# Selective scan on one core: one 1024-column scan over two channel quarters, with a zero decay standing at their border

## The chip, the cores and the metric

The kernel runs on one NeuronCore of one Trainium2 chip. The time is the device time of one execution in microseconds (us). Six instruction streams matter: PE (TensorE, matmuls), DVE (VectorE), ACT (ScalarE), POOL (GpSimd), SP (which issues most transfers), and the transfers themselves. Each engine works through its own queue in the order in which the program lists the instructions, and waits at the head of its queue until what the instruction needs is there.

## The reference, cut to what matters

Four layers run one after another: attention with group norm, a deformable convolution block, three residual convolution steps, and a four-direction state-space layer (Mamba). The change touches the last one only. For a token sequence of L = 4096 positions, 256 inner channels and 16 states per channel it computes

```python
dA  = jnp.exp(dt[..., None] * A)                         # decay, between 0 and 1
dBu = dt[..., None] * Bm[:, :, None, :] * xh[..., None]
def step(h, inp):
    dA_t, dBu_t = inp
    h = dA_t * h + dBu_t
    return (h, h)
_, hs = lax.scan(step, h0, (dA..., dBu...))              # h0 = 0
y = jnp.einsum('lbdn,bln->bld', hs, Cm)
```

for 2 images and 4 directions (rows and columns, each forward and flipped). The sequence starts at zero in each direction.

## The kernel before

**Tiling.** In `layer3` a block is 512 positions (`BLK`) of one direction of one image: 64 blocks, 8 per direction. The state goes from one block to the next of the same direction. Within a block the 256 channels fall into two halves (`hf`) of 128, and the 16 states into four sets (`ng`) of 4. A *group* is (block, half, set), so there are 8 groups in a block, and `slot` is the number of the group in its block. The 128 partitions of a group's tile hold 4 states x 32 channels; the four quarters `q` of a half's 128 channels lie side by side along the free dimension. The tile `db` (128 x 4 x 512) holds all of a group.

**What happens to a group.**
- `spread_store` and `spread_load` bring dt (and dt times u) by way of DRAM (`dx`) into the tile `dd4`, in which each channel's row stands four times.
- `db_dve` (L1518, the product at L1522) and `db_pool` (L1527, L1531) write the products dBu into `db`. The table `ND` (L1239) says how many of the 512 columns are DVE's; the rest are POOL's. Three groups have a POOL share: slot 1 and slot 6 entirely, slot 2 from column 176. DVE's share reads B from a PSUM tile `pbc`, which a matmul in `weights` (L1494, L1501) writes; POOL's reads a copy `b` fetched by SP.
- `expo` (L1541) lets ACT write the decays of one quarter into a PSUM tile `da` (L1544). There are three `da` buffers, and ACT runs two quarters ahead of DVE (`AHEAD`, L1695).
- `scan` (L1552, L1558) is one DVE instruction for 512 columns of one quarter. It reads `da` and `db` and writes the states into `db`. The state at the end of the block before enters in one of two ways: as the scan's starting value, read from `hl`, or, where `carried` (L1536) says so, by a small ACT instruction in `expo` (L1550) that adds decay times `hl` to the first column of `db`; the scan then starts from zero.
- `keep` (L1560, L1563) copies the last column to `hl` on ACT.
- `cmul` (L1565, L1568) multiplies the states by C on POOL, and `sums` (L1570, L1576) adds the states of a channel by small matmuls into `py`; `gate` (L1582, L1585) multiplies the result by the silu of z on DVE.

**What sets the order.** The layer is written under a manual schedule: each engine's queue has the order of the Python calls. The main loop (L1749) takes one group `k` per round. A round issues transfers for the next block, `weights(k + 2)`, then for each quarter an exponential (two quarters ahead) and a scan; then `db_dve(k + 1)`, `cmul(k - 1)`, `db_pool(k + 2)`; then one portion of the front of the next block by `slot` (`front_pe`, `front_act`, `front_pool`: projections, softplus, silu); and last `sums(k - 2)`. Among ACT's portions are `conv_silu` in slot 7 (L1409) and `zproj_silu` in slot 4 (L1422), each with two loads of the activation table, and `softplus` in slots 1 and 2. In some blocks one more tile of layer norm for a later block is worked in (13 in the main loop); its mean and variance take `da` buffers (`ln_tile`, L1320).

**PSUM** has 8 banks of 512 columns: `da` 3, `pbc` 2, `py` 1, and `pm3` 2 for all else in the layer.

Of the kernel before, what the change touches and what calls it, by code (L numbers as in the profile page):

```python
# [1229 lines left out]
def layer3(g, I, out):  # L1230
# [5 lines left out]
    nc, tc = g.nc, g.tc  # L1236
    NJ = 4

    ND = ((BLK, 0, 176, BLK), (BLK, BLK, 0, BLK))  # L1239
    NNG = N_STATE // NJ  # L1240
    HB = 1
    HC = 3
    with ExitStack() as ctx:
        a = ctx.enter_context(tc.tile_pool(name="l3a", bufs=1))
        dr = ctx.enter_context(tc.tile_pool(name="l3dr", bufs=2, space=bass.MemoryType.DRAM))
        psd = ctx.enter_context(tc.tile_pool(name="l3psd", bufs=3, space=PSUM))
        psb = ctx.enter_context(tc.tile_pool(name="l3psb", bufs=2, space=PSUM))
# [67 lines left out]
        xt = a.tile([P, L + 2 * HC], F32, name="xt")  # L1315
        N = {}
        NFIRST = 3


        def ln_tile():  # L1320

            return psd.tile([P, BLK], F32, name="da")

        def ln_mean(b, k):
            N[k, "mean"] = ln_tile()
            nc.tensor.matmul(N[k, "mean"], onesm, interior(g, b, k * RB, RB), start=True, stop=True)

        def ln_less(b, k):
# [10 lines left out]
            nc.scalar.activation(N[k, "sq"], N[k, "xc"], AF.Square)  # L1339

        def ln_var(b, k):
            N[k, "var"] = ln_tile()
# [42 lines left out]
        def reverse(i):  # L1385
            b, nd, _ = blocks[i]
            return dirs[b][nd][2]
# [91 lines left out]
        def spread_store(i, hf):  # L1479

            S[i]["dx", hf] = dr.tile([P, 2, BLK], F32, name="dx")
            nc.sync.dma_start(S[i]["dx", hf], S[i].pop(("dd", hf)))

        def spread_load(i, hf):
            s_ = S[i]
            dx = s_.pop(("dx", hf))
            dd4 = d4.tile([P, 2, 4, BLK], F32, name="dd4")
            for x in range(2):
                src = dx[:, x, :].rearrange("(q c) t -> c q t", c=32)
                for j in range(NJ):  # L1490
                    nc.sync.dma_start(dd4[32 * j : 32 * j + 32, x], src)
            s_["d4", hf] = dd4

        def weights(k):  # L1494

            i, hf, ng = groups[k]
            G[k] = {}
            if ND[hf][ng] == 0:
                return
            pb = psb.tile([P, BLK], F32, name="pbc")  # L1500
            nc.tensor.matmul(pb, sel[:, ng].rearrange("p j c -> p (j c)"), S[i]["bc"], start=True, stop=True)  # L1501
            G[k]["pb"] = pb
# [8 lines left out]
                nc.sync.dma_start(t[32 * j : 32 * j + 32], S[i]["bx"][r0 + j].partition_broadcast(32))  # L1511

        def db_tile(k):
            if "db" not in G[k]:
                G[k]["db"] = wk.tile([P, 4, BLK], F32, name="db")
            return G[k]["db"]

        def db_dve(k):  # L1518
            i, hf, ng = groups[k]
            n = ND[hf][ng]  # L1520
            if n:
                nc.vector.tensor_tensor(  # L1522
                    db_tile(k)[:, :, :n], G[k].pop("pb")[:, :n].unsqueeze(1).to_broadcast([P, 4, n]),
                    S[i]["d4", hf][:, 1, :, :n], ALU.mult,
                )
# [7 lines left out]
                    S[i]["d4", hf][:, 1, :, n:], ALU.mult,  # L1533
                )

        def carried(k, q):  # L1536

            i, hf, ng = groups[k]
            return i % NBLK > 0 and (q >= 2 or ND[hf][ng] == 0)

        def expo(k, q):  # L1541
            i, hf, ng = groups[k]
            da = psd.tile([P, BLK], F32, name="da")
            nc.scalar.activation(da, S[i]["d4", hf][:, 0, q, :], AF.Exp, scale=am[:, hf, q, ng : ng + 1])  # L1544
            G[k]["da", q] = da
            if carried(k, q):

                first = BLK - 1 if reverse(i) else 0
                b0 = G[k]["db"][:, q, first : first + 1]
                nc.scalar.activation(b0, da[:, first : first + 1], AF.Identity, bias=b0, scale=hl[:, hf, ng, q, :])  # L1550

        def scan(k, q):  # L1552
            i, hf, ng = groups[k]
            d0, d1 = G[k].pop(("da", q)), G[k]["db"][:, q, :]
            if reverse(i):
                d0, d1 = d0[:, ::-1], d1[:, ::-1]
            zero = i % NBLK == 0 or carried(k, q)
            nc.vector.tensor_tensor_scan(d1, d0, d1, 0.0 if zero else hl[:, hf, ng, q, :], ALU.mult, ALU.add)  # L1558

        def keep(k):  # L1560
            i, hf, ng = groups[k]
# [75 lines left out]
        def transfers(i, slot):  # L1637
            if i < NBK:
                if slot == 1:
                    bc_store(i)  # L1640
                elif slot == 4:
                    spread_store(i, 0)
                elif slot == 5:
                    spread_load(i, 0)
                    spread_store(i, 1)
            if slot == 0 and i - 1 < NBK:
                spread_load(i - 1, 1)
            for x, ahead in (("b", 4), ("c", 1)):
# [37 lines left out]
        with tc.manual_schedule():  # L1686
# [7 lines left out]
            units = [(k, q) for k in range(len(groups)) for q in range(4)]  # L1694
            AHEAD = 2  # L1695

            for k in range(NFIRST):
                ln_mean(0, k)
            for k in range(NFIRST):
# [34 lines left out]
            for ng in range(NNG):  # L1734
                copies(0, "b", ng)
                copies(0, "c", ng)
            for k in range(2):
                weights(k)
            db_dve(0)
            db_pool(0)  # L1740
            front_pe(0, 4)
            front_act(0, 4)
            front_pe(0, 5)
            front_pe(0, 6)
            for u in range(AHEAD):
                expo(*units[u])
            front_act(0, 7)
            db_pool(1)
            for k in range(len(groups) + 7):  # L1749
                i, slot = divmod(k, 8)  # L1750
                live = k < len(groups)
                more = k + 1 < len(groups)
                ended = 1 <= k <= len(groups)
                transfers(i + 1, slot)
                if k + 2 < len(groups):
                    weights(k + 2)
                norm = next_norm(i)
                for q in range(4):
                    if slot == 6 and q == 3 and 1 <= i <= NBK:
                        finish(i - 1)  # L1760
                    if norm and slot == 2 and q == 3:
                        ln_log(*norm)
                    if q == 0 and ended:
                        keep(k - 1)
                    if 4 * k + q + AHEAD < len(units):
                        expo(*units[4 * k + q + AHEAD])
                    if norm and q == 0:
                        if slot == 0:
                            ln_mean(*norm)
                        elif slot == 2:  # L1770
                            ln_var(*norm)
                    if live:
                        scan(k, q)

                    for j, hf in (((k - 6) // 8, 0), ((k - 10) // 8, 1)):
                        if q == 1 and 8 * j + 6 + 4 * hf == k and 0 <= j < NBK:
                            gate(j, hf)
                if norm and slot == 0:
                    ln_less(*norm)
                if more:  # L1780
                    db_dve(k + 1)
                if ended:
                    cmul(k - 1)
                if k + 2 < len(groups):
                    db_pool(k + 2)

                if slot == 5 and 0 <= k - 2 < len(groups):
                    sums(k - 2)
                if slot == 5 and 1 <= i <= NBK:
                    project(i - 1)  # L1790
                front_pe(i + 1, slot)
                front_act(i + 1, slot)
                front_pool(i + 1, slot)
                if norm:
                    if slot == 1:
                        ln_square(*norm)
                    elif slot == 3:
                        ln_root(*norm)
                    elif slot == 5:
                        ln_scale(*norm)  # L1800
                    elif slot == 6:
                        ln_store(*norm)
                if live:

                    if slot == 6 and 0 < i % (4 * NBLK) <= NBLK // 2:
                        for n in range(2):
                            turn(blocks[i][0], 2 * (i % (4 * NBLK) - 1) + n)

                if slot != 5 and 0 <= k - 2 < len(groups):
                    sums(k - 2)  # L1810


@with_exitstack
# [157 lines left out]
```

## Time and profile before

| | us |
|---|---|
| median of 3 runs | 5605.49 (5605.03 to 5607.73) |
| the profiled execution | 5610.11 |
| its span in the trace | 5608.3 |
| scan stage in the trace, first to last scan | 2309.25 to 5593.16 |
| DVE busy from 2309 to 5594 | 3207.1 |
| POOL busy there | 3236.5 |
| ACT busy there | 2777.5 |
| PE busy there | 2627.1 |

The profile is one execution. Its page gives the busy time of each engine, then the span in 40 slices with a digit for the busy tenths, then the chain of work that ended last, then groups of instructions: line, engine, operation, tiles (out<-in), shapes, count, then busy us in total and mean ns of one, then the engine's idle time just before them and what ended most of it. A timeline lists instructions by their start, with their length; `x2` stands for two merged neighbours. A table of stretches gives each engine's busy time between two points in time. A "wait" line says which instruction waited for which, with the total, the number of times and the longest.

### The profile page before, as it was taken

The page shows a single profiled execution, that of the slowest core. Times are in us where ns is not written, and L with a number is a line of the kernel's source. Part 1 is how long each engine was busy: PE and PEld are TensorE (multiplying, and loading weights), DVE is VectorE, ACT ScalarE, POOL GpSimd, SP SyncE. Part 2 cuts the span into 40 slices and gives each one's busy share as a digit, 9 for nine tenths or more (in the row PEclk, how much of TensorE's full clock was granted, in tenths as well). Part 3 has the DMA queues.
Part 4 walks back from the last instruction along what each step waited for, and adds up shares of the span by engine and source line. Part 5 has one row for each costly group of instructions (what it writes and reads, how often), then busy time and mean ns, then how long its engine had stood idle before and what let it go on. Part 6 is the DMA issues. An engine that isn't in the chain of part 4 may idle for free.

```text
span 5608.3 us, 54471 instructions
## 1 busy us (share of the span) xinstructions
PE 4731.0 (84%) x17062; PEld 1757.8 (31%) x17062; DVE 4537.0 (81%) x4232; ACT 4086.5 (73%) x6282; POOL 3661.7 (65%) x1197
## 2 busy tenths in 40 slices
PE   6999999899788699777788887878888888877786
PEld 3444444344344244222222222222222222222221
DVE  6566555552144998699999999999999999999998
ACT  3999999500255311698888888888888888888886
POOL 6222222100100311599999999999999999999999
PEclk8999999999899899888888888888878787888887
DMA  4111111300375000465565556556555655565554
GB/s 155 38 46 46 31 31 38 62 1 1 76 128 83 27 0 0 104 143 129 129 141 137 135 126 144 129 129 148 140 133 128 144 134 131 130 147 131 134 137 106
DMA packets 334569, 554.27 MB, mean 99 GB/s; under 512 B 69264, under 2 KB 115872, under 8 KB 334080
## 3 DMA queue, kind: packets, MB, share of 16 engines
q1 hardware_dynamic: 331136, 547.17, 41.2%
q10 hardware_dynamic: 3136, 3.56, 0.3%
q8 instruction: 135, 2.21, 0.2%
q14 instruction: 162, 1.33, 0.1%
HBM read 461.40 MB, written 89.13 MB: 98 GB/s over the span
## 4 chain that ended last, share of the span: by engine, by line
DVE 45%; PE 35%; ACT 11%; issue 5%; DMA 2%; POOL 1%; SPq 1%; DVEq 0%; ACTq 0%; POOLq 0%
DVE db L1558 30%; DVE db L1522 11%; PE ps L312 8%; PE acc L328 8%; PE m L1112 5%; PE m L600 5%; ACT da L1544 4%; PE acd L846 2%; ACT db L1550 1%; DVE gt L1585 1%; PE m L560 1%; ACT L1409 1%; ACT u L1409 1%; PE pf L809 1%; DMA hats<-pos 1%
## 5 line engine op out<-in xcount | busy, mean ns | idle before, releaser
L1568 POOL TENSOR_TENSOR db<-db,c 128x2048 f32<-128x2048 f32 x512 | 2314.0, 4535 | 48.3 <-ACT hl L1563 32.7
L1544 ACT ACTIVATE da<-dd,am 128x512 f32<-128x512 f32 x2048 | 1398.6, 687 | 300.4 <-DVE db L1558 281.6
L1558 DVE TENSOR_TENSOR_SCAN db<-da,db 128x512 f32<-128x512 f32 x1376 | 1585.2, 1204 | 36.3 <-ACT db L1550 28.1
L318 ACT ACTIVATE e<-ps 128x1536 f16<-128x1536 f32 (+1 forms) x683 | 919.0, 1624 | 7.9 <-PE ps L312 7.9
L1558 DVE TENSOR_TENSOR_SCAN db<-da,hl,db 128x512 f32<-128x512 f32 x672 | 825.9, 1271 | 41.6 <-POOL db L1531 2.6
L1522 DVE TENSOR_TENSOR db<-pbc,dd 128x2048 f32<-128x2048 f32 (+1 forms) x384 | 781.3, 2035 | 32.1 <-DMA dd<-dx 32.1
L1531 POOL TENSOR_TENSOR db<-b,dd 128x2048 f32<-128x2048 f32 (+1 forms) x192 | 773.5, 4029 | 12.7 <-DMA b<-bx 12.7
L1576 PE MATMUL py<-db,fold 128*32 128x512 f32 x4096 | 615.6, 687 | 153.2 <-POOL db L1568 153.1
L312 PE MATMUL ps<-q 128*128 128x512 f16 x2048 | 554.0, 379 | 4.3 <-DVE flag L260 2.7
L328 PE MATMUL acc<-e,v 128*128 128x512 f16 x2048 | 553.7, 379 | 0.1
L346 POOL TENSOR_TENSOR parts<-parts 32x512 f32<-32x512 f32 x64 | 80.6, 1259 | 707.5 <-DVE parts L345 707.5
L1550 ACT ACTIVATE db<-da,db,hl 128x1 f32<-128x1 f32 x1120 | 394.0, 352 | 146.7 <-DVE db L1522 103.2
L339 DVE RECIPROCAL rec<-acc 32x512 f32<-32x512 f32 x64 | 214.9, 3358 | 257.9 <-PE acc L328 248.3
L1112 PE MATMUL m<-v,u 128*128 128x512 f32 x864 | 379.3, 602 | 41.8 <-DVE v L1055 40.9
L1469 PE MATMUL pm<-dd,ident 128*128 128x512 f32 x512 | 359.7, 841 | 2.5 <-ACT dd L1462 2.5
L1428 PE MATMUL pm<-u,wxp 128*72 128x512 f32 x256 | 196.7, 913 | 141.0 <-ACT u L1409 141.0
L1501 PE MATMUL pbc<-bc,sel 64*128 64x512 f32 x384 | 208.3, 542 | 123.6 <-DVE db L1522 122.8
L312 PEld LDWEIGHTS <-q 128*128 128x128 f16 x2048 | 197.7, 97 | 278.5 <-issue 103.6
L328 PEld LDWEIGHTS <-v 128*128 128x128 bf16 x2048 | 199.3, 97 | 248.8 <-issue 10.2
L600 PE MATMUL m<-comb,w 64*128 64x512 f32 (+4 forms) x1296 | 269.9, 575 | 0.0
L720 POOL TENSOR_SCALAR yt<-y 32x512 f32<-32x512 f32 x8 | 18.1, 2268 | 380.8 <-DVE y L711 380.4
L1576 PEld LDWEIGHTS py<-db,fold 128*32 128x32 f32 x4096 | 90.6, 114 | 553.2 <-issue 306.7
(324 smaller groups left out, 6563.4 us busy)
## 6 DMA issues: line engine op xcount, KB each, us to landing
dd<-dx SPq DMA_DIRECT2D x1024, 256.0 KB, 6.5
dx<-dd SPq DMA_DIRECT2D x128, 512.0 KB, 5.4
c<-bx SPq DMA_DIRECT2D x1024, 64.0 KB, 2.1
hats<-pos SPq DMA_DIRECT2D x136, 256.0 KB, 9.8
b<-bx SPq DMA_DIRECT2D x512, 64.0 KB, 4.6
piece<-qd SPq DMA_DIRECT2D x128, 128.0 KB, 2.8
piece<-kd SPq DMA_DIRECT2D x112, 128.0 KB, 2.7
w<-in_conv0T SPq DMA_DIRECT2D x18, 288.0 KB, 8.5
```

What stands on the lines that cost most here:

```text
L312: nc.tensor.matmul(ps[:, i, :], t[:, 1, kb * P : (kb + 1) * P], t[:, 0, qb * BLK : (qb + 1) * BLK], start=True, stop=True,)
L318: nc.scalar.activation(e[:, :n, :], ps[:, :n, :], AF.Exp, scale=1.0 / UP**2)
L328: nc.tensor.matmul(acc, v3[b][:, kb, h, :], e[:, i, :], start=(kb == 0), stop=(kb == NS - 1))
L600: yield lambda q=q, dy=dy, src=src, i0=i0, i1=i1: nc.tensor.matmul(m[:, i0 * NF : i1 * NF], w[half, dy, q, x, :], src, start=(dy == KC and ...
L1112: nc.tensor.matmul(m[x], weights[j][:, dy, x, :], v[j][b][:, x, r0 : r0 + RP, :].rearrange("p r i -> p (r i)"), start=(dy == 0), stop=(dy ...
L1522: nc.vector.tensor_tensor(db_tile(k)[:, :, :n], G[k].pop("pb")[:, :n].unsqueeze(1).to_broadcast([P, 4, n]), S[i]["d4", hf][:, 1, :, :n], A ...
L1531: nc.gpsimd.tensor_tensor(db_tile(k)[:, :, n:], S[i]["b", ng][:, n:].unsqueeze(1).to_broadcast([P, 4, BLK - n]), S[i]["d4", hf][:, 1, :, n ...
L1544: nc.scalar.activation(da, S[i]["d4", hf][:, 0, q, :], AF.Exp, scale=am[:, hf, q, ng : ng + 1])
L1550: nc.scalar.activation(b0, da[:, first : first + 1], AF.Identity, bias=b0, scale=hl[:, hf, ng, q, :])
L1558: nc.vector.tensor_tensor_scan(d1, d0, d1, 0.0 if zero else hl[:, hf, ng, q, :], ALU.mult, ALU.add)
L1568: nc.gpsimd.tensor_mul(v, v, S[i]["c", ng].unsqueeze(1).to_broadcast([P, 4, BLK]))
L1576: nc.tensor.matmul(S[i]["y", hf][32 * q : 32 * q + 32, :], fold, G[k]["db"][:, q, :], start=False, stop=(ng == NNG - 1),)
```

## The change

It joins the quarters in pairs `p`. Two standing PSUM tiles `decays[0]` and `decays[1]` of 2 x 512 columns (four banks) take the place of the three `da` buffers, and `pbc` is left with one bank. One scan instruction runs over 1024 columns, the two quarters of a pair. At the border between the quarters the decay is a zero, so the second quarter starts anew. `border` writes that zero on DVE when the direction turns, and the exponentials leave that column out (511 columns in place of 512).

A scan can no longer take a starting value for each quarter, so all scans start from zero, and `carry` adds decay times last state to the first column of `db`: one DVE addition of 128 x 4 per group, in blocks that continue a direction. What it adds is worked out per half block: `first_load` fetches dt of the first position from `dx` (four small transfers), `first_decays` multiplies by A on POOL, `first_exp` takes the exponential on ACT, and `first_states` multiplies by `hl` on DVE. `carried`, the ACT patches and the scan's start from `hl` are gone.

POOL's share of slot 2 starts at column 320 in place of 176. `weights(k + 2)` moves from the start of a round to its end, and layer-norm tiles of the main loop move to `pm3`. Order in the round: `keep`, the scan of pair 0, the exponentials of the next group's pair 0, in slots 7, 2 and 3 a part of the new work, the gate, the scan of pair 1, the exponentials of pair 1, `db_dve`, `carry`.

```diff
-    ND = ((BLK, 0, 176, BLK), (BLK, BLK, 0, BLK))
+    ND = ((BLK, 0, 320, BLK), (BLK, BLK, 0, BLK))
...
-        psd = ctx.enter_context(tc.tile_pool(name="l3psd", bufs=3, space=PSUM))
-        psb = ctx.enter_context(tc.tile_pool(name="l3psb", bufs=2, space=PSUM))
+        psd = ctx.enter_context(tc.tile_pool(name="l3psd", bufs=1, space=PSUM))
+        psb = ctx.enter_context(tc.tile_pool(name="l3psb", bufs=1, space=PSUM))
...
+        decays = [psd.tile([P, 2, BLK], F32, name=f"da{p}") for p in range(2)]
+
+        def ln_tile(b, k):
+            if b == 0 and k < NFIRST:
+                return decays[k // 2][:, k % 2, :]
+            return psm.tile([P, BLK], F32, name="pm3")
...
+        def first_load(i, hf):
+            if i % NBLK:
+                first = BLK - 1 if reverse(i) else 0
+                src = S[i]["dx", hf][:, 0, first : first + 1].rearrange("(q c) t -> c (q t)", c=32)
+                df = S[i]["df", hf] = ck.tile([P, 4], F32, name=f"df{hf}")
+                for j in range(NJ):
+                    nc.sync.dma_start(df[32 * j : 32 * j + 32], src)
+
+        def first_decays(i, hf):
+            if i % NBLK:
+                e = S[i]["e", hf] = ck.tile([P, NNG, 4], F32, name=f"e{hf}")
+                nc.gpsimd.tensor_tensor(
+                    e, S[i].pop(("df", hf)).unsqueeze(1).to_broadcast([P, NNG, 4]),
+                    am[:, hf].rearrange("p q n -> p n q"), ALU.mult,
+                )
+
+        def first_exp(i, hf):
+            if i % NBLK:
+                nc.scalar.activation(S[i]["e", hf], S[i]["e", hf], AF.Exp)
+
+        def first_states(i, hf):
+            if i % NBLK:
+                e = S[i]["e", hf]
+                nc.vector.tensor_tensor(e, e, hl[:, hf].rearrange("p n q t -> p n (q t)"), ALU.mult)
+
+        def carry(k):
+
+            i, hf, ng = groups[k]
+            if i % NBLK:
+                first = BLK - 1 if reverse(i) else 0
+                b0 = G[k]["db"][:, :, first]
+                nc.vector.tensor_tensor(b0, b0, S[i]["e", hf][:, ng, :], ALU.add)
...
+        def border(p, rev):
+
+            x = BLK - 1 if rev else 0
+            nc.vector.memset(decays[p][:, 0 if rev else 1, x : x + 1], 0.0)
+
+        def expo(k, p):
 
             i, hf, ng = groups[k]
+            rev = reverse(i)
+            if k == 0 or reverse(groups[k - 1][0]) != rev:
+                border(p, rev)
+            for x in range(2):
+                r = slice(0, BLK)
+                if rev and x == 0:
+                    r = slice(0, BLK - 1)
+                elif not rev and x == 1:
+                    r = slice(1, BLK)
+                q = 2 * p + x
+                nc.scalar.activation(
+                    decays[p][:, x, r], S[i]["d4", hf][:, 0, q, r], AF.Exp, scale=am[:, hf, q, ng : ng + 1]
+                )
+
+        def scan(k, p):
+
             i, hf, ng = groups[k]
...
+            d0 = decays[p].rearrange("p x t -> p (x t)")
+            d1 = G[k]["db"][:, 2 * p : 2 * p + 2, :].rearrange("p x t -> p (x t)")
             if reverse(i):
                 d0, d1 = d0[:, ::-1], d1[:, ::-1]
-            zero = i % NBLK == 0 or carried(k, q)
-            nc.vector.tensor_tensor_scan(d1, d0, d1, 0.0 if zero else hl[:, hf, ng, q, :], ALU.mult, ALU.add)
+            nc.vector.tensor_tensor_scan(d1, d0, d1, 0.0, ALU.mult, ALU.add)
...
                 elif slot == 5:
+                    first_load(i, 0)
                     spread_load(i, 0)
                     spread_store(i, 1)
+                elif slot == 6:
+                    first_load(i, 1)
...
+                if ended:
+                    keep(k - 1)
...
+                if live:
+                    scan(k, 0)
+                if more:
+                    expo(k + 1, 0)
+                if slot == 7 and more:
+                    first_exp(i + 1, 0)
+                    first_states(i + 1, 0)
+                elif slot == 2 and live:
+                    first_exp(i, 1)
+                elif slot == 3 and live:
+                    first_states(i, 1)
+                for j, hf in (((k - 6) // 8, 0), ((k - 10) // 8, 1)):
+                    if 8 * j + 6 + 4 * hf == k and 0 <= j < NBK:
+                        gate(j, hf)
+                if live:
+                    scan(k, 1)
+                if more:
+                    expo(k + 1, 1)
...
                 if more:
                     db_dve(k + 1)
+                    carry(k + 1)
...
+                if slot == 6 and i + 1 < NBK:
+                    first_decays(i + 1, 0)
+                elif slot == 1 and live:
+                    first_decays(i, 1)
...
                 if slot != 5 and 0 <= k - 2 < len(groups):
                     sums(k - 2)
+                if k + 2 < len(groups):
+                    weights(k + 2)
```

More of the change, by code (lines that the diff above doesn't have):

```diff
@@ L1317, in layer3 @@
         NFIRST = 3
-        def ln_tile():
-            return psd.tile([P, BLK], F32, name="da")
+        decays = [psd.tile([P, 2, BLK], F32, name=f"da{p}") for p in range(2)]
[3 more added lines that the diff above has]
+            return psm.tile([P, BLK], F32, name="pm3")
         def ln_mean(b, k):
-            N[k, "mean"] = ln_tile()
+            N[k, "mean"] = ln_tile(b, k)
             nc.tensor.matmul(N[k, "mean"], onesm, interior(g, b, k * RB, RB), start=True, stop=True)
@@ L1341, in ln_var @@
         def ln_var(b, k):
-            N[k, "var"] = ln_tile()
+            N[k, "var"] = ln_tile(b, k)
             nc.tensor.matmul(N[k, "var"], onesm, N[k, "sq"], start=True, stop=True)
@@ L1492, in spread_load @@
             s_["d4", hf] = dd4
+        def first_load(i, hf):
[25 more added lines that the diff above has]
+                nc.vector.tensor_tensor(b0, b0, S[i]["e", hf][:, ng, :], ALU.add)
         def weights(k):
             i, hf, ng = groups[k]
-            G[k] = {}
+            G.setdefault(k, {})
             if ND[hf][ng] == 0:
@@ L1513, in db_tile @@
         def db_tile(k):
-            if "db" not in G[k]:
+            if "db" not in G.setdefault(k, {}):
                 G[k]["db"] = wk.tile([P, 4, BLK], F32, name="db")
@@ L1534, in db_pool @@
                 )
-        def carried(k, q):
+        def border(p, rev):
+            x = BLK - 1 if rev else 0
+            nc.vector.memset(decays[p][:, 0 if rev else 1, x : x + 1], 0.0)
+        def expo(k, p):
             i, hf, ng = groups[k]
-            return i % NBLK > 0 and (q >= 2 or ND[hf][ng] == 0)
-        def expo(k, q):
-            i, hf, ng = groups[k]
[L1543 to L1554, printed above, removed]
+            rev = reverse(i)
[12 more added lines that the diff above has]
+        def scan(k, p):
+            i, hf, ng = groups[k]
+            d0 = decays[p].rearrange("p x t -> p (x t)")
+            d1 = G[k]["db"][:, 2 * p : 2 * p + 2, :].rearrange("p x t -> p (x t)")
             if reverse(i):
                 d0, d1 = d0[:, ::-1], d1[:, ::-1]
-            zero = i % NBLK == 0 or carried(k, q)
-            nc.vector.tensor_tensor_scan(d1, d0, d1, 0.0 if zero else hl[:, hf, ng, q, :], ALU.mult, ALU.add)
+            nc.vector.tensor_tensor_scan(d1, d0, d1, 0.0, ALU.mult, ALU.add)
         def keep(k):
@@ L1693, in layer3 @@
             nc.vector.memset(xn[:, HB + HW, :HC], 0.0)
-            units = [(k, q) for k in range(len(groups)) for q in range(4)]
-            AHEAD = 2
             for k in range(NFIRST):
@@ L1736, in layer3 @@
                 copies(0, "c", ng)
-            for k in range(2):
-                weights(k)
+            weights(0)
             db_dve(0)
+            weights(1)
             db_pool(0)
@@ L1744, in layer3 @@
             front_pe(0, 6)
-            for u in range(AHEAD):
-                expo(*units[u])
+            for p in range(2):
+                expo(0, p)
             front_act(0, 7)
@@ L1754, in layer3 @@
                 transfers(i + 1, slot)
-                if k + 2 < len(groups):
-                    weights(k + 2)
                 norm = next_norm(i)
[L1758 to L1777, printed above, removed]
+                if ended:
+                    keep(k - 1)
+                if norm and slot == 0:
+                    ln_mean(*norm)
+                elif norm and slot == 2:
+                    ln_var(*norm)
+                if live:
[16 more added lines that the diff above has]
+                    expo(k + 1, 1)
+                if slot == 6 and 1 <= i <= NBK:
+                    finish(i - 1)
+                if norm and slot == 2:
+                    ln_log(*norm)
                 if norm and slot == 0:
```

## The prediction

> **What bounds the kernel now.** First the slices and totals, to find the stage. The lines below are from the page: the engine totals, two rows of the 40 slices, and the costliest groups.
>
> ```profile
> PE 4731.0 (84%) x17062; PEld 1757.8 (31%) x17062; DVE 4537.0 (81%) x4232; ACT 4086.5 (73%) x6282; POOL 3661.7 (65%) x1197
> ...
> DVE  6566555552144998699999999999999999999998
> ...
> POOL 6222222100100311599999999999999999999999
> ...
> L1568 POOL TENSOR_TENSOR db<-db,c 128x2048 f32<-128x2048 f32 x512 | 2314.0, 4535 | 48.3 <-ACT hl L1563 32.7
> ...
> L1558 DVE TENSOR_TENSOR_SCAN db<-da,db 128x512 f32<-128x512 f32 x1376 | 1585.2, 1204 | 36.3 <-ACT db L1550 28.1
> ...
> L1558 DVE TENSOR_TENSOR_SCAN db<-da,hl,db 128x512 f32<-128x512 f32 x672 | 825.9, 1271 | 41.6 <-POOL db L1531 2.6
> ```
>
> The change touches only the scan stage: the last 3285 us (first scan at 2309, last at 5593 us), 64 blocks of mostly 51.18 us. There DVE and POOL both sit at 9. Who leads? The table of stretches gives one block from 4864.47 us: DVE 50.11, POOL 50.43, ACT 43.46 us busy. Busy time alone does not settle it, so I ask who waits. DVE's waits in the stage, longest first, then its timeline over a block border:
>
> ```profile
> DVE db L1522 <- DMA dd<-dx: 32.1, 1, 32.1
> DVE db L1558 <- ACT db L1550: 29.4, 57, 1.4
> DVE db L1558 <- POOL db L1531: 2.6, 4, 1.0
> ```
>
> ```profile
> 4879.28 2.27 DVE L1522 TENSOR_TENSOR db<-pbc,dd 128x2048 f32<-128x2048 f32 x1
> 4881.66 2.46 DVE L1558 TENSOR_TENSOR_SCAN db<-da,hl,db 128x512 f32<-128x512 f32 x2
> 4884.07 4.57 DVE L1558 TENSOR_TENSOR_SCAN db<-da,db 128x512 f32<-128x512 f32 x4
> 4889.04 2.34 DVE L1558 TENSOR_TENSOR_SCAN db<-da,db 128x512 f32<-128x512 f32 x2 [0.40 <-ACT db L1550]
> 4891.30 0.87 DVE L1522 TENSOR_TENSOR db<-pbc,dd 128x704 f32<-128x704 f32 x1
> 4892.30 2.46 DVE L1558 TENSOR_TENSOR_SCAN db<-da,hl,db 128x512 f32<-128x512 f32 x2
> ```
>
> In a block DVE waits 0.40 us, for ACT's patch of the first column, and almost never for POOL (2.6 us in all). POOL's full product for slot 6 ends at 4863.8 while DVE reads it at 4867.2. So **DVE's own queue sets the pace**, with POOL a few us ahead.
>
> Two prices are read from this timeline. Independent DVE instructions overlap: four zero-start scans take 4.54 us where nothing disturbs them (4865.02), so a start-to-start step is (4.54 - 1.20) / 3 = 1.114, 0.085 under the 1.20 of one. Dependent ones do not: from product start (4879.28) to the scan that reads it (4881.66) are 2.38 us for a 2.27 us product, a gap of 0.107. Scans that start from hl step by 1.187 (2.46 pair; 2.37 to the next). One block by these steps: 14 x 1.187 + 18 x 1.114 + 5 x 2.375 + 0.975 + 2 gates x 0.58 = 50.7 us; with the 0.40 wait it is the block seen.
>
> **The change, part by part (us over the program; 56 of the 64 blocks continue a direction and carry states).**
>
> *Scans, -97.* 2048 go, 1024 of twice the length come. Before: 672 x 1.187 + 1376 x 1.114 = 2331. No 1024-column scan is in the trace. The two forms of the L1522 product, 704 columns in 0.867 us and 2048 in 2.268, give 1.042 ns a column and 0.133 us fixed. If a scan has the same fixed part, 512 columns cost 1.198 - 0.133 = 1.065, and the step is 1.114 + 1.065 = 2.18; 1024 x 2.18 = 2234. Ends: two whole steps, 2.228 (-49); a fixed part of 0.32, from the dearest short DVE row I found (the statistics aggregate of 48 columns, L945, 0.372 less 48 x 1.04 ns), 1.99 (-293). I take 2.18: the product is the nearest row, same engine, two inputs, one of them in PSUM.
>
> *Border column of the product moved from POOL to DVE, +38.* 144 columns x 4 = 576 elements x 1.042 ns = 0.60 us x 64. POOL loses 576 x 2.12 ns = 1.22 us a block (its 1344- and 2048-element forms, 3.034 and 4.527 us).
>
> *carry, +96.* One addition of 128x4 per group, on DVE between the product and the scan, both dependent. Small dependent DVE additions stand in an earlier layer:
>
> ```profile
> 1644.43 0.16 DVE L865 TENSOR_TENSOR af<-mv,af 128x2 f32<-128x2 f32 x1
> 1644.62 0.16 DVE L866 TENSOR_TENSOR af<-af 128x2 f32<-128x2 f32 x1
> 1644.82 0.16 DVE L867 TENSOR_TENSOR af<-af,mv 128x2 f32<-128x2 f32 x1
> ```
>
> A step of 0.195 for 0.16 busy: a gap of 0.035 with one wait, where the scan, which waits for ACT too, has 0.107. In the six groups with a DVE product: 0.035 + 0.16 + 0.107, less the 0.107 that stood there, about 0.20. In the two without, scan followed scan freely: 0.16 + 0.107 = 0.27. So 56 x (6 x 0.20 + 2 x 0.27) = 96. Ends: 0.08 each if all overlaps (36), 0.30 with the long gap twice (134).
>
> *Wait of first_states in slot 7, +92.* This is the step I rest most on. In slot 7 DVE's queue reads scan(k,0), first_states(i+1,0), scan(k,1). first_states needs first_exp on ACT; ACT has first_exp behind expo(k+1,0), which writes the decay tile that scan(k,0) reads. So DVE, at the end of scan(k,0), waits for the two exponentials and first_exp, and scan(k,1) and all after it stand behind. Price: DVE to ACT 0.04 (scan ends 4878.25, ACT starts 4878.29), two exponentials 1.29 (the x2 group at 4889.88), first_exp 0.12 beyond them (0.21, between the 128x4 copy's 0.193 and the 128x32 exponential's 0.231, less 0.09 overlap), 0.03 back to DVE, 0.08 step of first_states itself: 1.56, where the next scan would have started 0.085 before the end: 1.64 x 56 = 92. Nothing fills it: DVE is the bound and has no other order. Half 1 has its first_exp one slot earlier than its first_states, so only the step of 0.1 x 56 = 6 is paid.
>
> *ACT, -29.* 1120 patches (0.35 each) go, and with them DVE's 29 us of waits for L1550. 112 first_exp come. What is late next: exponentials are now written a pair at a time into two standing tiles, behind conv_silu in slot 7 (4879.00 to 4882.87, 3.87 us). From the end of scan(7,1): 1.33 + 3.87 + 0.2 (keep) = 5.4; the pair for slot 1 takes 1.3, so 6.7; DVE wants it after a product, carry and two scans, at about 7.3. It fits by 0.6, and zproj_silu in slot 4 likewise. I take 0 as new wait; the other end is all 29 back.
>
> *Covered, 0.* first_decays on POOL (0.184 fixed + 16 x 2.12 ns = 0.22, twice a block) against the 1.22 that POOL saves. first_load, 4 issues on SP of 0.46 us (8 dd<-dx take 3.64), makes dd4 of half 0 some 1.8 later: issued at 4908.97, landed by about 4919, read at about 4928. For half 1 SP waits some 5.4 us for the dx store, ahead of a copy of b; that one was issued by 4871.4 and is read by POOL at 4887.6. weights behind sums with one pbc buffer: between two products on DVE lie two scans and a carry, 4.6 us, for a 0.5 us matmul and what sums waits for POOL, which is ahead. Layer-norm tiles in pm3: 13 blocks only. Border memsets: 12 x 0.06. If PE's cover went, 0.5 x 6 x 64 = 190 would come.
>
> Sum: -97 + 38 + 96 + 92 + 6 - 29 = **+106**. The profiled execution took 5610.1 (span 5608.3), so 5716 on its scale; it lies 4.6 over the median of 5605.5, on which it is 5712.
>
> [...] Rows: a scan in a train costs 0.049 us beyond its columns (1.114 - 1.065), a carry 0.20 to 0.27. Of the -97, 49 come from the dearer start from hl and 48 from the halved count; with the carries' 96, count and carries make +48. [...]
>
> **Rivals.**
> - *Longer scans save far more: faster.* Place: the second half of each scan. It decides once the step is under 2.18 - 106/1024 = 2.08, a fixed part of some 0.23. At 0.32 (1.99): 106 - 196 = -90, 5516. For: a short DVE row reaches 0.37. Against: the product has 0.133, additions 0.16. Chance 0.07.
> - *The change does not make DVE wait in slot 7* (the pair and first_exp are done before DVE arrives). Then +14: 5620. Against: the decay tile has a single buffer and its reader is the scan just ahead. Chance 0.10.
> - *ACT or PE becomes the bound*: two tiles for three, one pbc buffer for two. If the 0.6 of margin goes over into a wait of 0.6 in slots 0 and 4 of each block: 64 x 1.2 = +77, 5789; with PE up to 5900. For: ACT's lead shrinks to one pair. Against: ACT sheds 1120 x 0.26 = 290 us. Chance 0.11.
> - *Forecast*: 5712, chance 0.72. Its low end takes the carries at 36 (-60): 5652. Its high end takes scans at 2.228 (+48) and the ACT waits back (+29): 5789.
>
> **How the numbers follow.** Range 5650 to 5790: the forecast's ends and most of the third rival; the first two and PE's tail, 2 in 10, stay out. Faster by over 0.2% (about what a measurement here tells from no change, 11 us): 0.07. Within: 0.05, half of the second rival. Slower: 0.88.
>
> **What would show it.** 1024 scans of 128x1024, mean about 2.27; 448 carries of 0.16; DVE waiting 56 times some 1.4 us for ACT's first_exp; a carrying block of about 53 us in place of 51.18, and one that starts a direction about 49.5; POOL's 128x768 product near 1.81 and POOL idle over 2 us a block; no wait for pbc. I am wrong if the scan's mean is under 2.15, if the wait on first_exp is missing, or if DVE waits for ACT's da or PE's pbc by tens of us.

## The result, and the profile after

The changed kernel takes 6540.72 us (median of 6 runs, 6530.85 to 6546.76) against 5606.06 (6 runs beside them): a ratio of 1.1665, 95% interval 1.165 to 1.168. The forecast was 5712, at most 5790. The direction was right, the size off by a factor of nine: +935 us in place of +106. The profiled execution has a span of 6542.5 us.

From the page of the changed kernel: the engine totals, three rows of slices, and the groups that answer to those shown of before (L1599 is the scan, L1526 carry, L1518 first_states, L1609 the product with C).

```profile
PE 4872.8 (74%) x17062; PEld 1786.7 (27%) x17062; DVE 5324.0 (81%) x3780; ACT 3831.2 (59%) x5274; POOL 3608.7 (55%) x1309
...
DVE  6656556413499689999999999999999999999998
ACT  4999995004541366665565666666656556555553
POOL 5222221000021177777777787877778777677676
...
L1609 POOL TENSOR_TENSOR db<-db,c 128x2048 f32<-128x2048 f32 x512 | 2313.8, 4520 | 888.3 <-ACT hl L1604 816.0
...
L1599 DVE TENSOR_TENSOR_SCAN db<-da,db 128x1024 f32<-128x1024 f32 x1024 | 2312.1, 2280 | 53.7 <-ACT da L1588 2.0
...
L1526 DVE TENSOR_TENSOR db<-db,e 128x4 f32<-128x4 f32 x448 | 539.1, 1203 | 10.6
...
L1518 DVE TENSOR_TENSOR e<-e,hl 128x16 f32<-128x16 f32 x112 | 305.3, 2726 | 91.7 <-ACT e L1513 91.7
```

DVE stays at 9 through the stage while POOL falls from 9 to 7: in the stage (2308 to 6526 us) POOL is busy 3183 of 4218 us, where it was 3236 of 3285. The scans cost what was forecast: 2.28 us each, where about 2.27 was expected. What stands out is that an addition of 4 columns has a *mean* of 1.20 us, and a product of 16 columns one of 2.73. They are counted as busy, not as waiting, so no list of waits names the cause. DVE's waits in the changed kernel hold the wait that was forecast, for first_exp (L1513), and one smaller surprise, for pbc:

```profile
DVE e L1518 <- ACT e L1513: 91.7, 56, 2.2
DVE db L1556 <- PE pbc L1535: 70.8, 43, 4.4
```

To see what stretches the additions, DVE's and POOL's timelines of the changed kernel are laid side by side (start, length):

```profile
5506.51 0.17 DVE L1526 TENSOR_TENSOR db<-db,e 128x4 f32<-128x4 f32 x1
...
5513.47 2.72 DVE L1526 TENSOR_TENSOR db<-db,e 128x4 f32<-128x4 f32 x1
...
5520.68 1.22 DVE L1526 TENSOR_TENSOR db<-db,e 128x4 f32<-128x4 f32 x1
...
5529.28 4.44 DVE L1526 TENSOR_TENSOR db<-db,e 128x4 f32<-128x4 f32 x1
```

```profile
5507.16 4.51 POOL L1609 TENSOR_TENSOR db<-db,c 128x2048 f32<-128x2048 f32 x1 [3.87 <-ACT hl L1604]
5511.63 4.53 POOL L1565 TENSOR_TENSOR db<-b,dd 128x2048 f32<-128x2048 f32 x1
5516.13 1.26 POOL L1478 TENSOR_TENSOR dd<-dd,u 128x512 f32<-128x512 f32 x1
5517.35 4.51 POOL L1609 TENSOR_TENSOR db<-db,c 128x2048 f32<-128x2048 f32 x1
...
5529.20 4.50 POOL L1609 TENSOR_TENSOR db<-db,c 128x2048 f32<-128x2048 f32 x1 [2.12 <-ACT hl L1604]
```

Add start and length. The first addition falls into a gap of POOL's (which is idle until 5507.16) and takes 0.17. The second ends at 5516.19, POOL's instruction at 5516.16; the third at 5521.90, POOL's at 5521.86; the fourth started 0.08 after a POOL instruction and ends at 5533.72, with POOL at 5533.70. Over the whole trace the additions take 0.14 to 4.45 us (the view of their line gives shortest, median and longest in ns):

```profile
L1526 DVE TENSOR_TENSOR db<-db,e x448: 138/724/4445, 2368.7 to 6518.9; 128x4 f32<-128x4 f32 x150
```

261 of the 448 take over 0.3 us (mean 1.94), and all of these end 0.02 to 0.03 us after a POOL instruction; the others take 0.18. Of the 112 products 100 are stretched, mean 3.04; they end 0.03 to 0.04 us after a POOL instruction.

**Theory:** a DVE instruction whose two tensor operands both lie in SBUF does not run beside POOL; it is held until POOL's running instruction ends. The scan (decays in PSUM), db_dve (pbc in PSUM), the gate (py in PSUM) and the layer-norm difference all read one operand from PSUM, so before the change DVE had no instruction of that kind in the stage, and this stage of its trace could show no hold (an earlier one does, see the part on why the prediction was wrong). **Rivals:** the additions are slow by their place (short, strided writes into a tile that POOL and ACT also touch) or by what they wait for; any short DVE instruction is slow beside POOL; the long scans or the new order of the round cost the time.

### The profile page after: what moved, and what is told of

It is laid out like the page before. It is cut to its first block, busy times and chain, and to the rows that moved or that the text cites. A ratio compares the mean times of both kernels' runs of the same rounds, so it can differ in the third digit from the quotient of the medians.

```text
span 6542.5 us, 53585 instructions
## 1 busy us (share of the span) xinstructions
PE 4872.8 (74%) x17062; PEld 1786.7 (27%) x17062; DVE 5324.0 (81%) x3780; ACT 3831.2 (59%) x5274; POOL 3608.7 (55%) x1309
## 4 chain that ended last, share of the span: by engine, by line
DVE 46%; PE 35%; issue 6%; DMA 4%; ACT 3%; POOL 3%; SPq 2%; DVEq 0%; ACTq 0%; POOLq 0%
DVE db L1599 25%; DVE db L1556 9%; PE ps L312 7%; PE acc L328 7%; DVE db L1526 6%; PE m L1112 5%; PE m L600 4%; DVE e L1518 3%; PE pm L1405 3%; PE acd L846 2%; DMA dd<-dx 1%; ACT da L1588 1%; DMA dx<-dd 1%; POOL db L1565 1%; POOL db L1609 1%
## 5 line engine op out<-in xcount | busy, mean ns | idle before, releaser
L1609 POOL TENSOR_TENSOR db<-db,c 128x2048 f32<-128x2048 f32 x512 | 2313.8, 4520 | 888.3 <-ACT hl L1604 816.0
L1588 ACT ACTIVATE da<-dd,am 128x512 f32<-128x512 f32 (+1 forms) x2048 | 1414.2, 691 | 1620.7 <-DVE db L1599 1547.1
L1599 DVE TENSOR_TENSOR_SCAN db<-da,db 128x1024 f32<-128x1024 f32 x1024 | 2312.1, 2280 | 53.7 <-ACT da L1588 2.0
L1556 DVE TENSOR_TENSOR db<-pbc,dd 128x2048 f32<-128x2048 f32 (+1 forms) x384 | 819.1, 2133 | 101.7 <-PE pbc L1535 70.8
L1565 POOL TENSOR_TENSOR db<-b,dd 128x2048 f32<-128x2048 f32 (+1 forms) x192 | 695.7, 3624 | 162.6 <-PE py L1617 73.3
L1535 PE MATMUL pbc<-bc,sel 64*128 64x512 f32 x384 | 224.3, 584 | 436.4 <-DVE db L1556 435.2
L1526 DVE TENSOR_TENSOR db<-db,e 128x4 f32<-128x4 f32 x448 | 539.1, 1203 | 10.6
L1405 PE MATMUL pm<-xt,wcs 128*128 128x512 f32 x512 | 301.4, 743 | 213.9 <-ACT hl L1604 150.3
L1405 PE MATMUL pm<-xn,wcs 128*128 128x512 f32 x512 | 291.8, 723 | 199.1 <-ACT res L1647 72.9
L1518 DVE TENSOR_TENSOR e<-e,hl 128x16 f32<-128x16 f32 x112 | 305.3, 2726 | 91.7 <-ACT e L1513 91.7
L1535 PEld LDWEIGHTS pbc<-bc,sel 64*128 64x128 f32 x384 | 82.1, 214 | 809.3 <-DVE db L1556 610.6
```

Of the source, the lines that this page charges most:

```text
L1405: nc.tensor.matmul(pu, wcs[:, hf, s, :], window(blk, sgn * s), start=(s == 0), stop=(s == 3))
L1526: nc.vector.tensor_tensor(b0, b0, S[i]["e", hf][:, ng, :], ALU.add)
L1556: nc.vector.tensor_tensor(db_tile(k)[:, :, :n], G[k].pop("pb")[:, :n].unsqueeze(1).to_broadcast([P, 4, n]), S[i]["d4", hf][:, 1, :, :n], A ...
L1565: nc.gpsimd.tensor_tensor(db_tile(k)[:, :, n:], S[i]["b", ng][:, n:].unsqueeze(1).to_broadcast([P, 4, BLK - n]), S[i]["d4", hf][:, 1, :, n ...
L1588: nc.scalar.activation(decays[p][:, x, r], S[i]["d4", hf][:, 0, q, r], AF.Exp, scale=am[:, hf, q, ng : ng + 1])
L1599: nc.vector.tensor_tensor_scan(d1, d0, d1, 0.0, ALU.mult, ALU.add)
```

## The experiments

**Taking the short instructions out.** The first leaves out the call of `carry`, the second the product in `first_states`, the third both.

```diff
-                    carry(k + 1)
...
-                nc.vector.tensor_tensor(e, e, hl[:, hf].rearrange("p n q t -> p n (q t)"), ALU.mult)
+                pass
```

> The changed kernel without the 448 additions of carry, so that no state enters a block (part of the computation is left out); first_states stays. Theory, held additions: a DVE instruction that reads two tensors from SBUF is held until POOL's running instruction ends. In the changed kernel's trace the 448 additions are busy 539 us, 467 more than 0.16 each; with the 96 that I had forecast for them unheld, 563 go: about 5980, and first_states keeps a mean of 2 to 3.5 us. Rival, small additions into the tile that POOL and ACT also touch are slow by their place in db: about 5980 too, but first_states, which touches no db, is then slow for another reason. Rival, the long scans themselves or the order of the round cost the time: it stays above 6400.

> The changed kernel without the 112 products of first_states (the last state is left out of what carry adds, part of the computation); carry stays. Held additions: 305 us of busy time less 112 x 0.16 = 287 go, with them the 92 of waits for first_exp in slot 7 and the 6 of steps: about 6155; the carries' mean stays above 1 us. Order of the round or the long scans: above 6400.

> The changed kernel without carry and without first_states (both left out, so no state passes between blocks); long scans, decay tiles, the new queue orders, the small transfers, first_decays and first_exp all stay. Held additions: 6540 - 563 - 385 = 5592, and down to 5520 if the 71 us in which DVE waits for pbc came from the holds too. If it is well above 5620, long scans or the new order cost by themselves.

Measured: without carry 5896 us (ratio 1.051, 1.048 to 1.054), without the product 6284 (1.120, 1.117 to 1.124), without both 5710 (1.018, 1.015 to 1.021). So 830 of the 935 us go with 560 instructions of 4 and 16 columns and with what waits on them, such as the 92 us for first_exp. None of the three times lies where it was expected (5980, 6155, 5592). The first two are under the rival's 6400; the third is over the 5620 from which the long scans or the order were to cost by themselves. The parts don't simply add: without carry the products' mean falls to 1.56 us (57 of the 112 stretched, in place of 100), and without the products the carries' busy time rises from 539 to 578 and the waits for pbc from 71 to 163. The long scans' own time is not the cause: it is 2.28 us each here too. But my sum without the short instructions was too low, 5592 against 5710, so about 100 us over the kernel before are owed to something else in the change. The waits of that run point to pbc:

```profile
DVE db L1556 <- PE pbc L1535: 167.5, 94, 4.9
...
DVE db L1599 <- POOL db L1565: 14.4, 16, 1.4
```

**Four probes in the kernel before.** Each adds 512 DVE instructions after the last scan of a group, reading data that is long there and writing a scratch tile that nobody reads. The four differ in their operands, and in the last two cases in the operation.

```diff
             nc.vector.tensor_tensor_scan(d1, d0, d1, ...)
+            if q == 3:
+                nc.vector.tensor_tensor(scr, am[:, 0, 0, :], am[:, 1, 0, :], ALU.mult)      # two_sbuf
+                nc.vector.tensor_tensor(scr, d0[:, 0:4], am[:, 1, 0, :], ALU.mult)          # one_psum
+                nc.vector.tensor_copy(scr, am[:, 0, 0, :])                                  # one_sbuf
+                nc.vector.tensor_reduce(scr[:, 0:1], am[:, 0, 0, :], AX.X, ALU.max)         # one_reduce
```

(One of the four lines each.)

> The kernel before, with one more DVE product of 128x4 per group (512 in all), from two constant SBUF tiles into a scratch tile, after the last scan of the group; nothing reads it and it waits for nothing but its own kind. Held additions: POOL is busy 98% of the stage with instructions of up to 4.5 us, so the product is held 1.2 (the mean that the carries had) to 2.2 us (half of POOL's long instruction): 5606 + 512 x 1.2 to 2.2 = 6220 to 6730, its end 0.03 us after the end of a POOL instruction. Rival, the additions of the change were slow through what they wait for or through their place in db: 0.16 each, 5650 to 5745.

> The kernel before with 512 more DVE products of 128x4, at the same place as in the run with two SBUF operands and into the same scratch tile, but with one operand in PSUM (the decays just read by the scan) and one in SBUF. Held additions: no holds, 0.15 to 0.20 each, 5606 + 512 x 0.08 to 0.27 = 5650 to 5745. Rival, any short DVE instruction is held while POOL runs: a mean of 1.2 and 6150 as with two SBUF operands.

> The kernel before with 512 more DVE copies of 128x4 from one constant SBUF tile into the scratch tile. If what holds is a second SBUF tensor operand: 0.06 to 0.20 each, 5625 to 5745. [...]

> The kernel before with 512 more DVE maxima over a row of 4 (128x4 to 128x1), SBUF to SBUF, at the place of the other probes. [...] If any DVE instruction between SBUF and SBUF is held: a mean near 1.2, some 6150.

Measured: 6150 us (1.096, 1.093 to 1.100), 5636 (1.005, 1.003 to 1.007), 6150 (1.096, 1.094 to 1.099) and 5632 (1.004, 1.002 to 1.005). The probes' own groups, one line from each run in that order; the last two numbers ahead of the idle time are busy us and mean ns:

```profile
L1561 DVE TENSOR_TENSOR scr<-am 128x4 f32<-128x4 f32 x512 | 611.9, 1195 | 0.0
```

```profile
L1561 DVE TENSOR_TENSOR scr<-da,am 128x4 f32<-128x4 f32 x512 | 69.0, 135 | 0.0
```

```profile
L1561 DVE COPY scr<-am 128x4 f32<-128x4 f32 x512 | 614.0, 1199 | 0.0
```

```profile
L1561 DVE TENSOR_REDUCE scr<-am 128x1 f32<-128x4 f32 x512 | 66.8, 130 | 0.0
```

The first two are the decisive pair: the same operation, place, size and destination cost 1.195 us with both operands in SBUF and 0.135 with one of them in PSUM. No dependence, no stride and no db is involved, so the rivals "by its place" and "any short instruction" fall. Of the 512 products with two SBUF operands 275 took over 0.3 us, mean 2.09, and nearly all of these ended 0.02 to 0.03 us after a POOL instruction. One of them, and POOL beside it (ends at 4515.33 and 4515.30):

```profile
4512.05 3.28 DVE L1561 TENSOR_TENSOR scr<-am 128x4 f32<-128x4 f32 x1
```

```profile
4510.78 4.52 POOL L1532 TENSOR_TENSOR db<-b,dd 128x2048 f32<-128x2048 f32 x1
```

The other 237 were not held, and POOL was busy 85% of this run's stage (2320 to 6120 us), not 98%: so 6150 lies under the 6220 to 6730 that was expected. The product with an operand in PSUM came out 14 us under its range. The copy, with a single operand, is held just as much (1.199 us on average), where 5625 to 5745 was expected if a second SBUF operand is what holds; the reduction, with a single operand too, is not (0.130), and its 5632 lies far under the 6150 that was expected if any instruction between SBUF and SBUF is held. So the count of tensors is not all. In these runs the held instructions have all operands in SBUF and write more than one column; what was not held reads a tensor from PSUM or writes one column. The runs do not show which property of the all-SBUF instructions decides, nor why a copy is held.

**The carry in another form, at its old place.** It becomes four instructions of one column each, whose other two operands are per-partition scalars in SBUF; the product of first_states goes, since hl enters here.

```diff
-                b0 = G[k]["db"][:, :, first]
-                nc.vector.tensor_tensor(b0, b0, S[i]["e", hf][:, ng, :], ALU.add)
+                for q in range(4):
+                    b0 = G[k]["db"][:, q, first : first + 1]
+                    nc.vector.tensor_scalar(
+                        b0, S[i]["e", hf][:, ng, q : q + 1], hl[:, hf, ng, q, :], b0, ALU.mult, ALU.add
+                    )
```

> The changed kernel with the carry at the same place in DVE's queue and into the same elements of db, but as four tensor_scalar instructions of 128x1 (e as the only tensor read, times hl plus the first column of db, both as per-partition scalars from SBUF); first_states goes, since hl enters here. [...] Rival, short writes into db are what is slow: as the changed kernel or more, over 6500. If a single column is held as the copies of 128x4 were: over 6300.

Measured: 6014 us (1.072, 1.070 to 1.074), under the 6300 that was expected of a held column and the 6500 of the rival. Its group:

```profile
L1527 DVE TENSOR_SCALAR db<-e,hl,db 128x1 f32<-128x1 f32 x1792 | 364.2, 266 | 16.1 <-POOL db L1568 0.7
```

Four times as many instructions into the same elements of db, none of them over 0.276 us, with POOL busy 86% of the time from 2320 to 5600 us: no holds, 526 us less than the changed kernel. This leaves nothing of the rival "by their place in db". The run is still slow: 364 us of DVE's time go to the short instructions, and 187 us to waits for pbc.

**The wait for pbc.** From the run without both short instructions, `weights(k + 2)` is put ahead of the front portion in PE's queue, first in every slot, then in slot 6 alone (the comments in the diff give the condition of the second).

```diff
+                if k + 2 < len(groups):                    # neither_slot6: and slot == 6
+                    weights(k + 2)
                 front_pe(i + 1, slot)
...
-                if k + 2 < len(groups):                    # neither_slot6: and slot != 6
-                    weights(k + 2)
```

> The run without carry and first_states (both left out again), with weights(k + 2) ahead of the front portion in PE's queue in place of behind sums; pbc keeps its one buffer. That run has 167 us of DVE waits for pbc. If PE's order makes them (the conv of slot 6, which waits for ACT, stands ahead of the matmul): most of 167 goes, 5550 to 5580. If the single buffer makes them: they stay, about 5700.

> The run without carry and first_states (both left out), with weights(k + 2) ahead of the front portion in slot 6 alone, where conv stands in PE's queue and waits for ACT. If that conv is what makes the matmul late: most of the 167 us of DVE waits for pbc go, 5550 to 5600. If the one buffer makes PE wait wherever the matmul is put (as in the run with it ahead in every slot, 6010): 5710 or more.

Measured: 6010 us (1.072, 1.069 to 1.074) and 5706 (1.017, 1.015 to 1.019). Neither gave the gain that I had put to PE's order, and 6010 is outside both cases of its expectation. In every slot, PE now stands 942 us (97 before) before pbc until DVE has read the single buffer, ACT waits for PE's part of the front (38 before), and DVE for POOL's products (14 before):

```profile
PE pbc L1535 <- DVE db L1556: 941.9, 238, 9.3
```

```profile
ACT dd L1473 <- PE pm L1470: 263.7, 128, 2.9
```

```profile
DVE db L1599 <- POOL db L1565: 343.1, 188, 3.3
```

In slot 6 alone DVE's wait goes elsewhere:

```profile
DVE db L1599 <- POOL db L1565: 140.8, 138, 2.7
DVE db L1556 <- PE pbc L1535: 39.5, 49, 1.7
```

167 + 14 became 40 + 141. So the conv of slot 6 did make most of the 167, but taking it out of the way brought a new wait in place of the old one. I read this as the one pbc buffer: PE cannot fetch B ahead, so whichever stands first in its queue, the other is late. That is not shown, because two buffers were not tried: the pools of the layer, with four banks for the decay tiles, stand at 8 banks again, as before.

**A long scan without short DVE instructions.** Each pair's scan starts from hl for its first quarter; ACT adds decay times state to the first column of the other (2 instructions per group), and the product stands between the two scans. `weights(k + 2)` moves ahead of the front portion in every slot, the place that costs 300 us in the run at 6010. No part of the computation is left out.

```diff
+                for p in range(2):
+                    q = 2 * p + (0 if rev else 1)
+                    b0 = G[k]["db"][:, q, first : first + 1]
+                    nc.scalar.activation(
+                        b0, S[i]["e", hf][:, ng, q : q + 1], AF.Identity, bias=b0, scale=hl[:, hf, ng, q, :]
+                    )
...
+            nc.vector.tensor_tensor_scan(d1, d0, d1, h0, ALU.mult, ALU.add)
...
+                if more:
+                    db_dve(k + 1)
+                    carry(k + 1)
+                    if k + 2 < len(groups):
+                        weights(k + 2)
```

> The long scans without any DVE instruction that has two SBUF operands: in each pair the scan starts from hl for its first quarter, and ACT adds decay times last state to the first column of the other quarter (2 instructions of about 0.35 per group; e comes from first_decays and first_exp as in the change). db_dve(k + 1) stands between the two scans of group k, so that ACT's additions lie beside a scan, and weights(k + 2) stands ahead of the front portion. By steps: 16 x (2.19 + 0.07) + 5 x 2.19 + 1.4 + 2 x 0.58 = 49.7 a block for DVE; POOL 50.4 - 1.2 + 0.4 = 49.6. Held additions: no holds, 64 x (49.7 - 51.2) = -96, so 5510, and up to 5570 with waits of a few tenths a block between two engines that are both full. Rival, long scans cost by something other than the additions: not under 5606.

Measured: 5959 us (1.063, 1.061 to 1.065), far over the 5510 to 5570 that was expected. DVE has no instruction left that could be held, but it waits for ACT's additions, 385 us where the whole loss is 350:

```profile
DVE db L1601 <- ACT db L1524: 385.1, 154, 5.1
```

Its timelines show where (two lines of DVE, four of ACT):

```profile
4526.86 2.35 DVE L1601 TENSOR_TENSOR_SCAN db<-da,hl,db 128x1024 f32<-128x1024 f32 x1 [2.53 <-ACT db L1524]
...
4548.98 2.35 DVE L1601 TENSOR_TENSOR_SCAN db<-da,hl,db 128x1024 f32<-128x1024 f32 x1 [3.58 <-ACT db L1524]
```

```profile
4521.31 1.28 ACT L1423 ACT_TABLE_LOAD   x1
...
4525.10 1.41 ACT L1588 ACTIVATE da<-dd,am 128x512 f32<-128x512 f32 x2
4526.45 0.65 ACT L1524 ACTIVATE db<-e,db,hl 128x1 f32<-128x1 f32 x2
...
4548.56 0.66 ACT L1524 ACTIVATE db<-e,db,hl 128x1 f32<-128x1 f32 x2 [0.79 <-POOL db L1565]
```

After slot 4 the silu of z with its table loads keeps ACT from 4521.31 to 4524.99, the pair and the addition for slot 6 follow, and DVE, which has no product of its own to do there, waits 2.53 us. At the next block border, after slot 7, it waits 3.58 us, of which ACT's addition itself spends 0.79 waiting for POOL's product (124 us over the run). A lead of one pair is not too short as such: in the run without both short instructions it is the same, and DVE waits 2.2 us for decays in all. What is new here is the additions, the product's place and the place of `weights`; no run takes the three apart, but the next run moves the product without the other two.

**The old scans with the product moved.** A last run asks whether order alone, without long scans, brings anything. POOL's share of slot 2 starts at column 240 here, the only other edit.

```diff
-    ND = ((BLK, 0, 176, BLK), (BLK, BLK, 0, BLK))
+    ND = ((BLK, 0, 240, BLK), (BLK, BLK, 0, BLK))
...
+                    if q == 1 and more:
+                        db_dve(k + 1)
...
-                if more:
-                    db_dve(k + 1)
```

> The kernel before (scans of 512) with two things only: db_dve(k + 1) stands between the second and third scan of group k, so that no scan waits for the product just ahead of it, and POOL's share of slot 2 starts at column 240. No short DVE instruction is added. A product then steps by 2.19 and not 2.375: DVE 50.7 - 6 x 0.19 + 0.27 = 49.8 a block, POOL 50.4 - 0.54 = 49.9. If DVE's queue was the bound as I read it: 64 x (50.0 - 51.2) = -77, 5530, and 5530 to 5590 with waits left. If POOL's queue was: 64 x 0.54 = 35 less, 5570. No gain: 5606.

Measured: 5803 us (1.034, 1.033 to 1.036), where 5530 to 5590 was expected, or 5606 if there was no gain. DVE waits 256 us for ACT's patches (29 before):

```profile
DVE db L1558 <- ACT db L1550: 256.0, 121, 2.4
```

I read this so: in the kernel before, the 2.3 us of the product after the fourth scan are also the time in which ACT makes up its lead. No run here beats the kernel before.

## Why the prediction was wrong, step by step

- **carry (+96) and first_states (its steps of 0.08 and 0.1, 10 us in all): the steps that failed.** Their prices came from L865 to L867, where POOL does nothing at all: between 1630 and 1660 us its busy time is 0.00. In the scan stage it was busy 98.5% of the time. The bounds, 36 to 134, were drawn from the same idle surroundings. Measured in the changed kernel, carries took 539 and products 305 us: 467 and 287 more than at 0.16 for each instruction, 754 of the 829 us that separate 6541 from 5712. The probe with two SBUF operands against the one with PSUM shows the hold by itself: 1.195 against 0.135 us. The trace of before had rows with the right neighbours as well; they stand below this list. Where POOL was first, the carries' holds end 0.02 to 0.03 us after POOL's instruction.
- **weights with one pbc buffer (0): failed by 71 us**, with the price I had named for a lost cover (up to 190) as the rival. The step had counted only `sums` ahead of the matmul in PE's queue; the conv of slot 6 stands there too. The two terms together, 754 + 71 = 825, account for the 829 us of error, though single terms are not known to 4 us. Without the holds this term grows: the terms left (-97, +38, -29) would give 5518, and the run without carry and first_states took 5710, with 167 us of waits for pbc. So even with no hold, and with no state passed on at all, it was some 100 us slower than the kernel before.
- **Scans (-97): held.** 2.280 us busy, 4.47 for two, so a step of 2.19 where 2.18 was estimated (1024 x 2.18 is 2232; the 2234 of the sum is a slip of 2 us). The rival of a dear fixed part falls.
- **Wait of first_exp in slot 7 (+92): held, and the match to the us is luck.** The page has 91.7 us in 56 waits, 1.64 each. Of the 1.64 in the sum only some 1.48 were wait; the rest was the product's step of 0.08 and the overlap lost.
- **POOL's smaller share and first_decays: held.** 1.809 us for the product of 768 columns (1.81 estimated), 0.225 us for first_decays (0.22).
- **ACT's -29: held.** DVE waits 2.0 us for decays in the changed kernel, and 2.2 in the run without carry and first_states, so this is not owed to the holds. The 385 us of the run with ACT's additions are waits for those, which the change had taken away.
- **"DVE's own queue sets the pace": true but too simple.** DVE and POOL were busy within 0.3 us of each other in the block (50.11 and 50.43), and ACT, with 43.46, has its work tied to moments between DVE's instructions. The run with `weights` ahead in slot 6 got a wait for POOL in place of the one that it lost, and the run with the product moved got one for ACT. (The block has 12 scans from hl and 20 from zero, not 14 and 18; by the same steps that is 50.5 us, not 50.7.)

**The rows of before that bear on carry.** First the stretch from which the prices came (after its length: busy us of PE, PEld, DVE, ACT and POOL), then, from the layer ahead of the scans, two differences of 256 columns with both operands from SBUF. They follow each other, in this form four times; the groups, then one place on DVE and on POOL:

```profile
1630.00:1660.00 30.00, 14.95 (x122) 8.20 (x120) 11.53 (x24) 16.28 (x22) 0.00 (x0) 0.77 0.57 104
```

```profile
L1060 DVE TENSOR_TENSOR t<-v 128x256 f32<-128x256 f32 x4 | 9.3, 2326 | 0.0
...
L1059 DVE TENSOR_TENSOR t<-v 128x256 f32<-128x256 f32 x4 | 1.7, 424 | 0.0
```

```profile
1855.07 0.43 DVE L1059 TENSOR_TENSOR t<-v 128x256 f32<-128x256 f32 x1
1855.40 3.06 DVE L1060 TENSOR_TENSOR t<-v 128x256 f32<-128x256 f32 x1
```

```profile
1855.24 2.94 POOL L1093 TENSOR_TENSOR v<-v,gt 128x1024 f32<-128x1024 f32 x1 [5.78 <-DVE v L1086]
```

The difference that starts after POOL's instruction takes 3.06 us and ends at 1858.46, 0.28 after POOL's 1858.18; the same operation ahead of it takes 0.43. So the hold could be read from this trace before the change. What a held instruction still needed after POOL's end was 0.02 us for 4 columns, 0.03 for 16 and, in this one case, 0.28 for 256.

## What to carry to other kernels

Before pricing a DVE instruction, ask what POOL does beside it: here, with POOL busy most of the stage (85% in the run with two SBUF operands), a DVE instruction of 4 columns that reads two tensors from SBUF, or copies one SBUF tensor to another, took 1.2 us on average, and nearly all the held products ended 0.02 to 0.03 us after POOL's running instruction. Take prices from rows with the same neighbours, not just the same shape; one operand in PSUM (0.135 us on average), or one column with per-partition scalars in place of a second tensor (0.266), kept it free of holds here. Where engines hand tiles to one another and two are nearly full, a saving on one can come back as a wait for the next: with `weights` ahead in slot 6, 167 us of waits for pbc and 14 for POOL became 40 and 141.

## What the runs showed of the hardware that was not expected

- A held instruction counts as busy. The sign is a mean far above the smallest of its kind (0.14 to 4.45 us for the carries) and ends that coincide with another engine's.
- A copy of 128x4 between SBUF tiles is held as much as a product of two (1.199 and 1.195 us on average), a reduction over the same 4 columns is not (0.130), nor a tensor_scalar of one column with two per-partition scalars from SBUF (0.266).
- A scan over the 1024 columns of a decay tile, two buffers of 512 side by side, took 2.280 us, where 2.27 was estimated from rows that read at most 512 columns of PSUM: no cost shows where the one meets the other.
